# The first block's normalisation moved behind its transposes: x turned by TensorE as it lands, the tokens' scale and bias spread by products with diagonals

## The chip, the core and the metric

The kernel runs on one core of one Trainium2 chip. Five engines work side by side, each through its own list of instructions in a fixed order: TensorE (PE; its weight loads are shown as PEld), VectorE (DVE), ScalarE (ACT), GpSimd (POOL) and SyncE (SP), which here issues most of the transfers. The metric is device time in microseconds (us) of one execution. Three runs of the kernel before gave 2379.66, 2381.79 and 2385.01 us; the median is 2381.79.

## The reference

Two layers over x of shape (2, 4096, 512), float32. Each layer normalises x over its 512 channels and adds the results of two branches to x:

```
xn = (x - mean(x)) / sqrt(var(x) + 1e-5)                     # per token
x1 = xn @ w1.T + w1_b ;  v = silu(xn @ v1.T + v1_b)          # layer 0
y  = ssm(silu(depthwise_conv3(x1)))
x  = x + (y * v) @ w2.T + w2_b + mx_quantised(xn) @ mx_quantised(weight).T + bias
xn = normalised(x)                                           # layer 1
x  = x + linear_attention_with_layernorm(xn) + token_mix_ffn(xn)
```

The change lies at the very beginning: the normalised x of the first 512 tokens, and its first two products, with w1 and v1.

## The kernel before

The 8192 tokens are worked in `NK` = 16 blocks of `T` = 512. Channels are held in `CC` = 4 chunks of 128 partitions, tokens of a block in `TJ` = 4 tiles of 128.

**Phase 1** (`block_kernel`, L1013 to L1102) runs over the 16 blocks. For each, `projected` (L345) makes 32 products of 128x128 weights with 128x512 of `xnT`, the block's normalised x with channels on partitions: four output chunks for w1, then four for v1, four products each, that is over the four channel chunks. In the trace each float32 product of this kind is two entries, so a block is 64 entries. The results go to PSUM banks taken in turn by the generator `banks` (L84) from three tags: `acc` (4 banks), `mm` (2) and `tr` (2), eight in all. ScalarE empties them: L357 adds w1's bias, L372 applies silu with v1's bias. VectorE and ScalarE then do the convolution's taps (`tapped`, L400: L403, L405, L412, L414) and, beside this, the quantisation of other tiles (`quantised`, L384). After phase 1 follow the recurrence and, for each of the two sequences, the mixing of layer 0 and all of layer 1.

**How xnT is made.** For blocks 1 to 15, x is loaded a second time in another layout (`laid`, L317, tile `xi`); ScalarE normalises it in 16 pieces of 128x128 (`laid_normalised`, L173, recorded at L134, four pieces for each 128 tokens), and VectorE transposes it 32 by 32, one instruction for each 128 tokens (L330). The mean and the reciprocal deviation come from the plain x (`fetched`, L292, ten tiles in a ring): `measured` (L299) runs BN_STATS and BN_AGGREGATE over four tiles and a chain of small instructions (L114 to L122, L146), with one square root on ScalarE (L116). `spread_out` (L136) brings these numbers into the other layout: one store to DRAM (`sd`) and four loads (`mvi`). All of a block's xnT has to be there before its first output chunk is complete.

For block 0 there is no time for that way. `first_turned` (L305) normalises the plain tiles on VectorE (L310, four instructions), TensorE transposes them (`transposed`, L150, sixteen transposes into four banks, L154), and ScalarE copies the four banks to xnT (L155).

**What sets the order.** The source is not the order of execution. A scheduler of the framework puts the instructions into one list per engine by its own estimates; each list is then strictly in order, and an instruction that waits holds up all behind it. `tc.issue_after(i)`, used in the change, forces what is issued under it to stand behind instruction i. Transfers on SP's queue also wait for an earlier transfer that used the same of eight semaphores.

In the lists of the kernel before, ScalarE has, after the first block's four w1 evictions: five of block 1's sixteen L134 pieces, the silu of v1's chunk 0, two pieces, chunk 1's silu, six pieces, chunk 2's silu, three pieces, a square root, and only then chunk 3's silu. VectorE has the four transposes of block 1 (L330) between BN_STATS of the x tiles of blocks 3, 4 and 5; those wait for transfers that SP issues late.

## Time and profile before

| | |
|---|---|
| median of the runs | 2381.79 us (2379.66 to 2385.01) |
| the profiled execution's own time | 2385.64 us |
| its span | 2383.8 us |
| TensorE busy | 2353.4 us, 99% of the span |
| VectorE, ScalarE, GpSimd busy | 1530.4, 1012.4, 479.2 us |
| TensorE's first transpose | at 9.73 us |
| TensorE's first product of block 0 | at 14.05 us |
| its last of block 0 ends | at 43.57 us |
| its first of block 1 | at 45.43 us |

Times in the timeline are microseconds from the start of the span: start, length, engine, line, operation, output and inputs, shape, number of instructions in the row; in brackets, how long the engine had been idle and what ended that. PEld rows are weight loads; products follow one another at the spacing of their loads. A row "SPq" or "ACTq" is the issue of a transfer, not the transfer. Because TensorE is busy 99% of the span, what matters is where it is not: the list of waits below is read for TensorE alone.

### The profile page before, as it was taken

Reading aid. Unit: us, or ns where it says so; the run is one execution under the profiler, and the core shown is the slowest. Engines: PE = TensorE matmul, PEld = TensorE weight load, DVE = VectorE, ACT = ScalarE, POOL = GpSimd, SP = SyncE. Lnnn points to the kernel's source line nnn. Section 1 sums busy time; section 2 is a strip of 40 time slices with the busy share of each in tenths; the row PEclk is TensorE's granted clock in tenths of the full one; section 3 lists DMA queues with packets and bytes.
Section 4 is the critical chain, followed back from the end, with each engine's and each line's share of the span. In section 5 each row is a group of like instructions: output and inputs, shape, how many; then the busy total and the mean of one; then the engine's idle time right before and its main releaser. Section 6 shows DMA issues by size and latency. Waiting matters only on the chain. (4 is left out here: it accounts for less than half of the span.)

```text
span 2383.8 us, 21961 instructions
## 1 busy us (share of the span) xinstructions
PE 2353.4 (99%) x6400; PEld 1104.5 (46%) x6400; DVE 1530.4 (64%) x3050; ACT 1012.4 (42%) x1929; POOL 479.2 (20%) x534
## 2 busy tenths in 40 slices
PE   7999999999999999999999999999999999999999
PEld 3444434466444444444445555444444444445554
DVE  6898765554576554266769779666553265567777
ACT  5785675344333233236663222233333246652222
POOL 0121210121243332100112112233332100001111
PEclk9999999999999999999999999999999999999999
DMA  7954433568734432212274445434332212254331
GB/s 246 303 138 142 142 133 115 158 198 288 290 107 119 115 110 86 62 44 97 93 252 164 141 141 194 154 111 120 111 117 65 62 40 80 97 212 142 129 132 57
DMA packets 253833, 328.12 MB, mean 138 GB/s; under 512 B 55953, under 2 KB 117393, under 8 KB 252689
## 3 DMA queue, kind: packets, MB, share of 16 engines
q1 hardware_dynamic: 224624, 259.59, 34.7%
q10 hardware_dynamic: 29088, 67.12, 7.2%
q8 instruction: 51, 0.84, 0.2%
q14 instruction: 70, 0.57, 0.1%
HBM read 205.38 MB, written 121.27 MB: 137 GB/s over the span
## 5 line engine op out<-in xcount | busy, mean ns | idle before, releaser
L704 PE MATMUL p_acc<-k,x 128*128 128x512 f32 x512 | 229.9, 592 | 0.9 <-ACT k L739 0.9
L160 PE MATMUL p_acc<-w_W_v,t 128*128 128x512 f32 x512 | 222.3, 592 | 0.0
L160 PE MATMUL p_acc<-w_W_r,xnT 128*128 128x512 f32 x448 | 201.4, 592 | 0.0
L160 PE MATMUL p_tr<-w_Wk,xnT 128*128 128x512 f32 x448 | 199.2, 592 | 0.1
L977 POOL TENSOR_TENSOR x<-x,row_beta 128x512 f32<-128x512 f32 x64 | 83.9, 1311 | 552.7 <-ACT xn L134 542.6
L673 PE MATMUL p_mm<-w_w_w,t 128*128 128x512 f32 x416 | 186.7, 592 | 0.0
L116 ACT ACTIVATE rs_s<-rs_v 128x4 f32<-128x4 f32 (+1 forms) x41 | 8.3, 205 | 393.7 <-DVE rs_v L114 393.6
L658 PE MATMUL p_mm<-w_d,t 128*128 128x512 f32 x384 | 173.6, 593 | 1.4 <-DVE x L681 1.2
L702 POOL TENSOR_TENSOR ksum<-ksum,k 128x512 f32<-128x512 f32 x62 | 83.3, 1344 | 369.2 <-ACT k L739 369.2
L704 PEld LDWEIGHTS p_acc<-k,x 128*128 128x128 f32 x512 | 97.2, 190 | 123.7 <-issue 120.8
L160 PEld LDWEIGHTS p_acc<-w_W_v,t 128*128 128x128 f32 x512 | 97.3, 190 | 122.5 <-issue 119.3
L738 DVE TENSOR_TENSOR k<-p_tr,row_bk 128x512 f32<-128x512 f32 x64 | 43.8, 684 | 162.1 <-PE p_tr L160 162.1
L983 ACT ACTIVATE r<-p_acc 128x512 f32<-128x512 f32 x64 | 38.2, 597 | 248.3 <-PE p_acc L160 236.3
L405 DVE SCALAR_TENSOR_TENSOR xc<-x,col_conv_w,xc 128x512 f32<-128x512 f32 x128 | 95.7, 763 | 65.8 <-ACT xc L403 33.5
L160 PEld LDWEIGHTS p_tr<-w_Wk,xnT 128*128 128x128 f32 x448 | 85.0, 190 | 107.6 <-issue 104.0
L186 POOL TENSOR_TENSOR xq<-xq,mx_rs 128x512 f32<-128x512 f32 x64 | 76.4, 1194 | 268.6 <-DVE mx_rs L185 205.7
L739 ACT ACTIVATE k<-k 128x512 f32<-128x512 f32 x64 | 40.1, 627 | 202.9 <-DVE k L738 198.5
L673 PEld LDWEIGHTS p_mm<-w_w_w,t 128*128 128x128 f32 x416 | 79.0, 190 | 99.5 <-issue 99.5
L134 ACT ACTIVATE xq<-xq,mvi 128x128 f32<-128x128 f32 x256 | 104.2, 481 | 44.0 <-DMA xq<-in_xi 43.0
L160 PE MATMUL p_acc<-xnT,w_w_w 128*128 128x512 f32 x256 | 117.3, 601 | 4.6 <-ACT x L357 2.1
L681 DVE TENSOR_TENSOR x<-x,p_mm 128x512 f32<-128x512 f32 x52 | 35.5, 683 | 133.3 <-PE p_mm L673 133.2
L160 PEld LDWEIGHTS p_acc<-w_W_r,xnT 128*128 128x128 f32 x448 | 80.8, 190 | 80.4 <-issue 80.4
(235 smaller groups left out, 4375.7 us busy)
## 6 DMA issues: line engine op xcount, KB each, us to landing
x<-in_x SPq DMA_DIRECT2D x126, 256.0 KB, 3.6
xq<-in_xi SPq DMA_DIRECT2D x64, 256.0 KB, 4.4
vd<-v ACTq DMA_DIRECT2D x64, 256.0 KB, 2.4
cd<-xs SPq DMA_DIRECT2D x64, 256.0 KB, 2.0
xg<-cd SPq DMA_DIRECT2D x16, 1024.0 KB, 6.8
v<-vd SPq DMA_DIRECT2D x64, 256.0 KB, 4.6
xd<-x SPq DMA_DIRECT2D x64, 256.0 KB, 2.0
qd<-q ACTq DMA_DIRECT2D x64, 256.0 KB, 2.0
```

The costliest lines, as they stand in the source:

```text
L134: nc.scalar.activation(dst, src, AF.Identity, bias=mv[:, 0:1], scale=mv[:, 1:2])
L160: nc.tensor.matmul(out_ap, lhsT=lhsT(k), rhs=rhs(k), start=(k == 0), stop=(k == CC - 1))
L186: nc.gpsimd.tensor_tensor(by_block(y), by_block(y), rs.unsqueeze(2).to_broadcast([P, NQ, QB]), ALU.mult)
L405: nc.vector.scalar_tensor_tensor(xc, x1[:, cc, tap : tap + T], conv_w[:, cc, tap : tap + 1], xc, ALU.mult, ALU.add,)
L658: nc.tensor.matmul(po, lhsT=xds[i][j][:, k, :], rhs=wd[:, k, :], start=(k == 0), stop=False)
L673: nc.tensor.matmul(po, lhsT=z[:, k, j * P : (j + 1) * P], rhs=w2[:, k, :], start=False, stop=(k == CC - 1),)
L702: nc.gpsimd.tensor_tensor(ksum, ksum, kt, ALU.add)
L704: nc.tensor.matmul(pg[c], lhsT=xn[:, c * P : (c + 1) * P], rhs=kt, start=first, stop=last)
L738: nc.vector.tensor_tensor(kt, pk, bk, ALU.add)
L739: nc.scalar.activation(kt, kt, AF.Relu)
L977: nc.gpsimd.tensor_tensor(xt[j], xt[j], beta, ALU.add)
L983: nc.scalar.activation(r, pr, AF.Sigmoid)
```

## The change

For block 0 alone, the order of normalising and transposing is turned round. TensorE transposes the plain x tiles as they land, into the four `acc` banks, one for each channel chunk. The tokens' scale and bias now have to vary along the free axis, the same on all partitions. They are made so by products: identity times a token's scale on its partition (a diagonal, made on VectorE for the scale and on ScalarE for the bias), multiplied from the left by a matrix of ones, gives a 128x512 tile whose every row holds the 512 tokens' values. ScalarE copies the scale's tile to SBUF; the bias's stays in a `tr` bank. VectorE then multiplies and adds chunk by chunk, eight instructions over 128x512, and forces the order multiply, add, multiply, add. The first two w1 outputs of block 0 are accumulated in turns, channel chunk by channel chunk. The order of bank tags in `banks` changes for all of phase 1, and the two small mask reductions are put behind the last of the eight instructions.

```diff
-            for tag in ("acc", "mm", "acc", "tr"):
+            for tag in ("mm", "tr", "acc", "acc"):
                 yield bank(tag, 4 if tag == "acc" else 2)
...
     def first_turned(work, xts):
         xnT = work.tile([P, CC, T], F32, tag="xnT", name="xnT")
-        xn = work.tile([P, TJ, D], F32, tag="xi", name="xn")
+        pxs = [acc() for _ in range(CC)]
         for j in range(TJ):
-            nc.vector.tensor_scalar(
-                xn[:, j, :], xts[j], mv0[:, 0, j, 1:2], mv0[:, 0, j, 0:1], ALU.mult, ALU.add
-            )
-        for j in range(TJ):
-            transposed(xnT[:, :, j * P : (j + 1) * P], xn[:, j, :], ("tr", "mm")[j % 2])
-        return xnT
+            for c in range(CC):
+                nc.tensor.transpose(
+                    pxs[c][:, j * P : (j + 1) * P], xts[j][:, c * P : (c + 1) * P], ident
+                )
+        measured(0, xts)
+        full = work.tile([P, P], F32, tag="xe", name="full")
+        nc.gpsimd.memset(full, 1.0)
+        wide = {}
+        for k, tag in ((1, "mm"), (0, "tr")):
+            diagonal = work.tile([P, TJ, P], F32, tag="xi", name="diagonal")
+            wide[k] = bank(tag)
+            for j in range(TJ):
+                if k:
+                    nc.vector.tensor_scalar(
+                        diagonal[:, j, :], ident, mv0[:, 0, j, k : k + 1], None, ALU.mult
+                    )
+                else:
+                    nc.scalar.activation(
+                        diagonal[:, j, :], ident, AF.Copy, scale=mv0[:, 0, j, k : k + 1]
+                    )
+                nc.tensor.matmul(
+                    wide[k][:, j * P : (j + 1) * P], lhsT=full, rhs=diagonal[:, j, :],
+                    start=True, stop=True,
+                )
+        scale = work.tile([P, T], F32, tag="xe", name="scale")
+        nc.scalar.copy(scale, wide[1])
+        shifted = None
+        for c in range(CC):
+            with tc.issue_after(shifted.ins) if c else nullcontext():
+                nc.vector.tensor_tensor(xnT[:, c, :], pxs[c], scale, ALU.mult)
+            shifted = nc.vector.tensor_tensor(xnT[:, c, :], xnT[:, c, :], wide[0], ALU.add)
+        return xnT, shifted
...
     def projected(work, n, xnT, before):
...
+        if not n:
+            two = [next(eight) for _ in range(2)]
+            for k in range(CC):
+                for o in range(2):
+                    nc.tensor.matmul(
+                        two[o], lhsT=w1[:, k, o * P : (o + 1) * P], rhs=xnT[:, k, :],
+                        start=(k == 0), stop=(k == CC - 1),
+                    )
         for o in range(CC):
-            pm = next(eight)
-            product(pm, lambda k: w1[:, k, o * P : (o + 1) * P], lambda k: xnT[:, k, :])
+            if not n and o < 2:
+                pm = two[o]
+            else:
+                pm = next(eight)
+                product(pm, lambda k: w1[:, k, o * P : (o + 1) * P], lambda k: xnT[:, k, :])
...
-            measured(0, xts[0])
-            xnT = first_turned(work, xts.pop(0))
+            xnT, shifted = first_turned(work, xts.pop(0))
...
-            nc.vector.tensor_reduce(mask, ...)     # two reductions, mask and mask_c
+            with tc.issue_after(shifted.ins):
+                nc.vector.tensor_reduce(mask, ...)
```

The lists that result differ from those before in phase 1 alone; from the recurrence on, each engine's list holds the same instructions in the same order. What is new in the lists around the first two blocks:

- VectorE: four diagonals; multiply, add for chunks 0 and 1; multiply for chunk 2, one BN_STATS of block 1, add; multiply for chunk 3, BN_AGGREGATE, a second BN_STATS of block 1, add; then the rest of block 1's statistics, with the masks among them. The fourth transpose of block 1 stands behind BN_STATS of the fourth x tile of block 4 and the first two of block 5.
- ScalarE: four diagonals, the copy of the scale, then the first w1 eviction, the square root for block 1, the other w1 evictions and taps, the square root for blocks 2 and 3, and then: silu of v1's chunk 0, one of block 1's sixteen pieces, silu 1, six pieces, silu 2, five pieces, silu 3, four pieces.
- TensorE: sixteen transposes, four products for the scale, four for the bias, then for each channel chunk one product for each of the first two outputs, with one product of the third output ahead of channel chunk 3's.
- SP: the transfers of x for block 3 stand around the store of block 1's statistics and ahead of its four loads. The stores and loads of the statistics of blocks 2 and 3 come ahead of most x tiles of blocks 4 and 5.
- GpSimd: one more memset ahead of the making of the identity.

More of the change, by code (lines that the diff above doesn't have):

```diff
@@ L1 @@
 from collections import defaultdict
-from contextlib import ExitStack
+from contextlib import ExitStack, nullcontext
 from functools import partial
@@ L1036, in block_kernel @@
             mask = const.tile([P, QC], F32, name="mask")
-            nc.vector.tensor_reduce(
-                mask, ident.rearrange("p (q t) -> p q t", q=QC), AX.X, ALU.add
-            )
             mask_c = const.tile([P, QC], F32, name="mask_c")
-            nc.vector.tensor_reduce(
-                mask_c, ident.rearrange("p (u q s) -> p q u s", u=2, q=QC), AX.XY, ALU.add
-            )
+            with tc.issue_after(shifted.ins):
+                nc.vector.tensor_reduce(
+                    mask, ident.rearrange("p (q t) -> p q t", q=QC), AX.X, ALU.add
+                )
+                nc.vector.tensor_reduce(
+                    mask_c, ident.rearrange("p (u q s) -> p q u s", u=2, q=QC), AX.XY, ALU.add
+                )
             x1 = None
```

## The prediction

> **What bounds the kernel now.** I read the page's first part, then TensorE's list of waits, then the timeline of the first 46 us, where the change lies.

> ```profile
> PE 2353.4 (99%) x6400; PEld 1104.5 (46%) x6400; DVE 1530.4 (64%) x3050; ACT 1012.4 (42%) x1929; POOL 479.2 (20%) x534
> ```

> TensorE is busy all the span: a gain must be a gap that TensorE loses, a loss one that it gets. Its gaps are few (line, who released it, us in total, times, longest):

> ```profile
> PE p_tr L154 <- DVE xn L310: 9.7, 1, 9.7
> ...
> PE p_acc L160 <- ACT x L357: 2.1, 1, 2.1
> ...
> PE p_acc L160 <- DVE xnT L330: 1.9, 1, 1.9
> ...
> PE p_acc L160 <- ACT xnT L155: 0.7, 1, 0.7
> ```

> The change works on the first, the last and, through block 1, the third. The second belongs to a group of four waits between 304 and 332 us (0.55, 0.17, 0.22 and 2.06, together 3.0), where ScalarE empties banks so late that all eight are full.

> ```profile
> 8.39 0.28 DVE L1037 TENSOR_REDUCE mask<-ident 128x4 f32<-128x128 f32 x1
> ...
> 9.04 1.91 DVE L310 TENSOR_SCALAR xn<-x,mv 128x512 f32<-128x512 f32 x4
> ...
> 9.73 1.09 PE L154 MATMUL p_tr<-ident,xn 128*128 128x128 f32 x4 [9.73 <-DVE xn L310]
> ...
> 13.41 0.59 ACT L155 COPY xnT<-p_mm 128x512 f32<-128x512 f32 x1 [0.27 <-PE p_mm L154]
> ...
> 14.05 5.48 PE L160 MATMUL p_acc<-xnT,w_w_w 128*128 128x512 f32 x8 [0.68 <-ACT xnT L155]
> ...
> 15.06 0.69 DVE L129 BATCH_NORM_STATS2 st<-x 128x6 f32<-128x512 f32 x1 [4.10 <-DMA x<-in_x]
> ...
> 16.78 0.34 PEld L160 LDWEIGHTS p_acc<-xnT,w_w_w 128*128 128x128 f32 x1 [0.52 <-issue]
> ...
> 17.63 0.21 PEld L160 LDWEIGHTS p_acc<-xnT,w_w_w 128*128 128x128 f32 x1 [0.52 <-issue]
> 18.08 0.19 PEld L160 LDWEIGHTS p_acc<-xnT,w_w_w 128*128 128x128 f32 x1 [0.24 <-issue]
> 18.51 0.19 PEld L160 LDWEIGHTS p_acc<-xnT,w_w_w 128*128 128x128 f32 x1 [0.24 <-issue]
> ...
> 39.97 3.60 PE L160 MATMUL p_tr<-xnT,w_v_w 128*128 128x512 f32 x8
> 40.17 0.69 ACT L372 ACTIVATE v<-p_acc,col_v_b 128x512 f32<-128x512 f32 x1 [0.30 <-PE p_acc L160]
> ...
> 44.70 0.68 DVE L330 STREAM_TRANSPOSE xnT<-xi 128x512 f32<-128x512 f32 x1
> ...
> 45.43 3.70 PE L160 MATMUL p_acc<-xnT,w_w_w 128*128 128x512 f32 x8 [1.86 <-DVE xnT L330]
> ```

> To be seen: product entries follow each other every 0.855 us (16.78 to 17.63) until some 17.9, then every 0.43. TensorE starts at half rate, though the granted clock shown for these stretches is 1.00; I go by the spacing. Block 0 is 64 entries: at 0.429 they take 27.46, and the half-rate time from 14.05 to 17.9 adds half of 3.85, so 14.05 + 27.46 + 1.93 + 0.1 = 43.5 (seen: 43.57). Block 1 waits 1.86 more: its last transpose stands in VectorE's list behind BN_STATS that wait for x tiles.

> **The change, part by part.**

> *Start of block 0.* Removed from the path: L310, the transposes behind it, the copies. The sixteen transposes now wait only for x (first BN_STATS at 4.60) and the identity (1.68, plus 0.20 for the added memset on GpSimd); at the old spacing, 0.215 each, they end near 8.1, beside the statistics, which take until 9.0. Cost nothing; without that cover they would cost their 3.4. Moving the two masks out of the chain of small VectorE instructions brings 0.1: 8.9.

> VectorE's four diagonals (128x128): the rows nearest are a TENSOR_SCALAR of 128x64 at 0.19 and L310's 128x512 at 0.48. I take 0.2, nearer in size; the first is done at 9.1 and TensorE starts at 9.25. Each of the eight products is float32, so two entries, of 128 columns: a quarter of 0.855, 0.21 at half rate, 0.11 at full. The scale's four end at 9.25 + 1.71 = 10.96, the bias's at 12.67 (at full rate 1.7 earlier; with 0.48 diagonals 0.5 later). ScalarE's diagonals cost 0.40 each by L134's 128x128 pieces, 9.0 to 10.6: beside TensorE's work. Copy of the scale: 0.59, to 11.65. Multiply and add have the row of another float32 product and sum out of PSUM:

> ```profile
> L738 DVE TENSOR_TENSOR k<-p_tr,row_bk 128x512 f32<-128x512 f32 x64 | 43.8, 684 | 162.1 <-PE p_tr L160 162.1
> ```

> 0.684 each. Chunk 0: multiply 11.67 to 12.35, add from 12.75 (the bias's products) to 13.43. First w1 entry: 13.5, against 14.05. So the gain at the start is 0.55, not the 5 us by which the transposes move.

> Chunks 1, 2 and 3 follow at 14.85, 16.7 and 18.65: 1.35 each, plus one BN_STATS (0.66, and up to 0.4 of waiting, its tile landing at 15.06) ahead of chunk 2's add and of chunk 3's. TensorE needs 3.4 for a chunk's two products at half rate (four entries) and 1.7 at full, so while cold it is behind the chunks: no stall. Were it warm from the start, chunk 3 would leave 50 entries for after 18.65: end at 40.6, the lower bound for block 0.

> *The clock.* Unknown: when full rate comes. Before, the transposes had been running from 9.73 and the change of spacing still came only 3.85 after the first true product. I take the same moment, 17.9. Then block 0 ends at 13.5 + 27.46 + 2.2 + 0.1 = 43.26, 0.3 earlier than 43.57. Latest bound: twice that half-rate time, 7.7 from 13.5, and an end of 44.9.

> [...]

> *Start of block 1: the added wait.* In the new list ScalarE has four of block 1's sixteen pieces behind the last silu of block 0, and that silu waits for block 0's last product. Before, no piece stood there. So from the end E of block 0: silu starts at E + 0.04 and holds ScalarE 0.59 (40.17 to 40.76); four pieces, 0.51 for the first (a transfer is issued behind it), 0.40, 0.40, 0.48: E + 2.4; VectorE's fourth transpose 0.69; to TensorE 0.05: E + 3.2, against 1.86 before. With E = 43.26: 46.45, against 45.43. **Loss 1.0.** Queued behind these pieces are block 2's sixteen and block 1's first eviction; 6.4 + 1.6 us of them bring that eviction to 53, and TensorE, with eight banks, needs its bank only a block later.

> Were E as early as 40.6, another wait would end last: the fourth transpose stands behind BN_STATS of three x tiles. Their transfers are issued behind the statistics of blocks 2 and 3. By my reckoning: first eviction 23.2; square root; block 1's statistics 25.4 (before 24.99); the x tiles of block 3 by 31; square root 32.1; statistics of blocks 2 and 3 33.2 (before 48.3); eight loads to 39.2; tiles issued to 40.5, landing some 3 later. The transpose can't start before 44.2: TensorE at 45.0, a gain of 0.4. With E = 44.9, 48.1: a loss of 2.7. So −0.4 to +2.7 here.

> *VectorE's load*: eight times 0.684 and four times 0.2, less 1.91: 4.4 us more before 20, where VectorE idles 19 of the first 45. Nothing, if cover remains (third rival).

> *SP*: two x tiles of block 2 now wait for transposes too (done at 8.1, issued at 14). The four x tiles of block 3 cost about 0.45 each ahead of block 1's loads; these wait for their store to land anyway.

> *The rest of phase 1.* Bank tags rotate over the same eight banks: nothing. The lists differ up to some 330 us, and the 3.0 of waits there may vanish or double; the same pile-up of quantisation ahead of silus and evictions stands in the new list, so I take 0, bounds −3.0 and +3.0. Afterwards the lists are equal and everything shifts.

> **Sum** against the profiled execution's 2385.64 (span 2383.8): −0.3 + 1.3 + 0 = +1.0. That execution is 3.85 above the median of the runs, as slow as their slowest, so the change is put on the median: 2381.79 + 1.0 = 2382.8.

> **Rivals.** *First (slower): block 1 waits for a transfer.* The square root of blocks 2 and 3 now stands ahead of block 0's first silu and of all sixteen pieces, and needs four x tiles. I have them by 31; the slowest x transfer in the first 60 us took 9.5 from issue to landing, 6 more than I assume. Then the square root comes at 38, the tiles ahead of the fourth transpose 6 later, at 50, and TensorE starts block 1 at 51.4: +6.0, 2387.8. It decides from 3 us of lateness on, where ScalarE's chain (silus, pieces and issues, 9.2) outlasts block 0. For it: TensorE's start then hangs on two landings in a row. Against: the median landing there was 4.8, and these transfers meet few others.

> *Second (faster, or the same): the gain is kept.* Full rate comes with the diagonals' products, block 1 starts at 45.0, and the new order is rid of the four waits: −0.4 − 3.0 = −3.4, 2378.4. Against: two independent strokes of luck.

> *Third: VectorE's 4.4 us are not covered.* At 304 to 332 TensorE waits for evictions that hang on VectorE; if that lateness has piled up since the start, the whole 4.4 arrives there, and block 1's gap is absorbed by it: 2386.2. Against: VectorE is busy for only 4.30 of the 10 us from 70 to 80.

> That the change doesn't do what it says is excluded: the transposes head TensorE's new list and wait for x and the identity alone.

> **How the numbers follow.** 0.2%, 4.8 us, is about what a measurement of this kernel can tell; the three runs shown spread over 5.4. Forecast 0.60 (own range 2380.5 to 2385.5), first rival 0.14, second 0.12, third 0.14. Faster by over 0.2% (under 2377.0): 0.05 from the second, 0.02 from the forecast. Slower (over 2386.6): 0.11, 0.05 and 0.02 from the first, third and forecast: 0.18. Same: 0.75. The range goes to the second's and the first's price, 2378.4 to 2387.8.

> **What would show it.** Right: transposes from 4.6 to 8.1, a gap, products at 9.3, first w1 entry near 13.5 with spacing 0.855; then block 1 released by the fourth transpose, ScalarE's four pieces directly ahead. Wrong: half spacing gone before 14; a wait for x ahead of the first silu; TensorE's waits of 304 to 332 gone or grown.

## The result, and the profile after

Five runs of the changed kernel took 2393.93 to 2397.61 us, median **2396.7**; the kernel before, on the same chip, 2381.79. The ratio is 1.0057, 95% interval 1.0047 to 1.0068: slower by 14.9 us, 9 over the top of the range on record. The profiled executions stand 8.3 apart only (2393.93 against 2385.64): the one of the changed kernel is the fastest of its five, that of the kernel before lies 3.9 above its median. So the account below is of 8.3 us, and what a slower execution of the changed kernel adds is read from a second profile.

The page's first part of the changed kernel, and TensorE's list of waits (us in total, times, longest us):

```profile
PE 2359.3 (99%) x6416; PEld 1108.9 (46%) x6416; DVE 1539.8 (64%) x3058; ACT 1013.9 (42%) x1931; POOL 476.7 (20%) x535
```

```profile
PE p_acc L313 <- DMA x<-in_x: 4.7, 1, 4.7
PE p_mm L160 <- DVE mv L130: 4.3, 1, 4.3
PE p_mm L160 <- DVE xnT L358: 4.3, 1, 4.3
...
PE p_acc L160 <- ACT x L397: 2.6, 2, 2.1
...
PE p_tr L160 <- ACT x L397: 1.1, 1, 1.1
```

Two waits of 4.3 us are new. The timeline says where they lie (start, length; in brackets the idle time before and what ended it):

```profile
4.71 3.65 PE L313 MATMUL p_acc<-ident,x 128*128 128x128 f32 x16 [4.71 <-DMA x<-in_x]
...
9.11 2.08 PE L332 MATMUL p_mm<-diagonal,full 128*128 128x128 f32 x8 [0.75 <-DVE diagonal L325]
...
13.68 1.13 PE L387 MATMUL p_mm<-xnT,w_w_w 128*128 128x512 f32 x2 [0.78 <-DVE xnT L342]
...
42.23 0.69 DVE L129 BATCH_NORM_STATS2 st<-x 128x6 f32<-128x512 f32 x1 [0.73 <-DMA x<-in_x]
...
43.55 0.69 DVE L129 BATCH_NORM_STATS2 st<-x 128x6 f32<-128x512 f32 x1 [0.41 <-DMA x<-in_x]
...
44.96 0.69 DVE L358 STREAM_TRANSPOSE xnT<-xi 128x512 f32<-128x512 f32 x1
...
45.71 6.05 PE L160 MATMUL p_mm<-xnT,w_w_w 128*128 128x512 f32 x8 [4.29 <-DVE mv L130]
```

The start is as drawn. TensorE then runs out of block 0 at 41.42 (45.71 less 4.29) and waits: the fourth transpose of block 1 stands behind statistics whose x tiles are still landing. (The list names L130, which ends 0.06 us behind the transpose.) The eight entries after the wait need 6.05 us instead of 3.7. In the same execution's windows, the column after POOL is the granted clock:

```profile
40.00:45.00 5.00, 1.41 (x4) 0.34 (x2) 3.00 (x7) 4.26 (x11) 0.00 (x0) 0.86 0.93 307
45.00:50.00 5.00, 4.29 (x5) 1.85 (x6) 4.77 (x14) 5.00 (x14) 0.00 (x0) 0.50 1.03 365
50.00:60.00 10.00, 10.00 (x24) 4.52 (x23) 8.44 (x20) 7.81 (x18) 1.36 (x3) 0.98 0.95 334
```

Behind the gap the clock stood at half, from 43.64 to 50.47 by its record, and behind the second gap again, from 217.72 to 221.14. That gap is at block 7, on VectorE (first fence before, second after):

```profile
202.01 0.67 DVE L182 TENSOR_REDUCE mx_s<-w_y 128x16 f32<-128x512 f32 x1
...
205.01 2.48 DVE L330 STREAM_TRANSPOSE xnT<-xi 128x512 f32<-128x512 f32 x4
...
208.00 0.38 DVE L194 TENSOR_SCALAR w_c<-w_y 128x512 int32<-128x512 int32 x1
```

```profile
207.88 1.25 DVE L194 TENSOR_SCALAR w_c<-w_y 128x512 int32<-128x512 int32 x1
...
209.14 0.67 DVE L182 TENSOR_REDUCE mx_s<-w_y 128x16 f32<-128x512 f32 x1
...
213.13 1.25 DVE L194 TENSOR_SCALAR w_c<-w_y 128x512 int32<-128x512 int32 x1 [0.94 <-POOL w_y L186]
214.42 0.43 DVE L197 TENSOR_SCALAR w_c<-w_c 128x512 f32<-128x512 f32 x1
214.76 2.48 DVE L358 STREAM_TRANSPOSE xnT<-xi 128x512 f32<-128x512 f32 x4
```

Before, one instruction on the tiles `w_y` and `w_c` (the quantisation of the weight for the mixing of layer 0, hundreds of us away) stood ahead of block 7's four transposes; in the new list seven do, with a wait for GpSimd among them. Four other transposes of VectorE that nothing needs so soon (table `ta`, see a_free) moved nearer to block 7 as well, from 182 to 195 us to 193 to 206. Block 6 ends at 213.12 and block 7 cannot begin:

```profile
217.39 5.37 PE L160 MATMUL p_mm<-xnT,w_w_w 128*128 128x512 f32 x8 [4.27 <-DVE xnT L358]
223.81 3.70 PE L160 MATMUL p_tr<-xnT,w_w_w 128*128 128x512 f32 x8 [1.06 <-ACT x L397]
227.99 7.13 PE L160 MATMUL p_acc<-xnT,w_w_w 128*128 128x512 f32 x16 [0.47 <-ACT x L397]
...
340.90 7.13 PE L160 MATMUL p_acc<-xnT,w_w_w 128*128 128x512 f32 x16 [2.10 <-ACT x L397]
```

The account of the profiled pair, after less before: block 0 ends 2.15 earlier (41.42 against 43.57); block 1 starts 0.28 later (45.71 against 45.43); half rate behind the gap, 6.05 − 3.7 = 2.4 by 51; at block 7, 4.27 + 1.06 + 0.47 of waits and 1.7 of half rate, 7.5; the four waits at 304 to 332 (3.0) are one of 2.10, −0.9. Sum 9.3. The recurrence's first products come at 476.21 against 467.07, **+9.14**; from there the lists are equal, and 0.8 comes back.

### The profile page after: what moved, and what is told of

Read it like the earlier page. It is cut to its first block, busy times and chain, and to the rows that moved or that the text cites. A ratio compares the mean times of both kernels' runs of the same rounds, so it can differ in the third digit from the quotient of the medians.

```text
span 2392.1 us, 22005 instructions
## 1 busy us (share of the span) xinstructions
PE 2359.3 (99%) x6416; PEld 1108.9 (46%) x6416; DVE 1539.8 (64%) x3058; ACT 1013.9 (42%) x1931; POOL 476.7 (20%) x535
## 4 chain that ended last, share of the span: by engine, by line
PE 69%; DVE 4%; issue 1%; ACT 1%; POOL 1%; DMA 0%; POOLq 0%; ACTq 0%; DVEq 0%
PE p_acc L160 18%; PE p_tr L160 9%; PE p_acc L744 8%; PE p_mm L713 7%; PE p_mm L698 7%; PE p_mm L869 6%; PE p_acc L869 6%; PE p_tr L869 2%; PE p_mm L996 1%; PE p_tr L996 1%; PE p_acc L698 1%; PE p_acc L534 1%; PE p_acc L713 1%; PE p_acc L544 1%; PE p_tr L713 1%
## 5 line engine op out<-in xcount | busy, mean ns | idle before, releaser
L160 PE MATMUL p_acc<-w_W_v,t 128*128 128x512 f32 x512 | 222.3, 592 | 0.0
L160 PE MATMUL p_acc<-w_W_r,xnT 128*128 128x512 f32 x448 | 201.4, 592 | 0.0
L160 PE MATMUL p_tr<-w_Wk,xnT 128*128 128x512 f32 x448 | 199.2, 592 | 0.2 <-ACT xnT L155 0.2
L160 PEld LDWEIGHTS p_acc<-w_W_v,t 128*128 128x128 f32 x512 | 97.3, 190 | 122.5 <-issue 119.3
L778 DVE TENSOR_TENSOR k<-p_tr,row_bk 128x512 f32<-128x512 f32 x64 | 43.8, 684 | 162.1 <-PE p_tr L160 162.1
L445 DVE SCALAR_TENSOR_TENSOR xc<-x,col_conv_w,xc 128x512 f32<-128x512 f32 x128 | 94.1, 752 | 69.1 <-ACT xc L443 35.9
L160 PEld LDWEIGHTS p_tr<-w_Wk,xnT 128*128 128x128 f32 x448 | 85.0, 190 | 107.7 <-issue 104.0
L134 ACT ACTIVATE xq<-xq,mvi 128x128 f32<-128x128 f32 x256 | 105.2, 481 | 43.7 <-DMA xq<-in_xi 41.6
L160 PEld LDWEIGHTS p_acc<-w_W_r,xnT 128*128 128x128 f32 x448 | 80.8, 190 | 80.4 <-issue 80.4
L160 PE MATMUL p_acc<-xnT,w_w_w 128*128 128x512 f32 x256 | 113.0, 593 | 2.6 <-ACT x L397 2.6
```

What stands on the lines that cost most here:

```text
L134: nc.scalar.activation(dst, src, AF.Identity, bias=mv[:, 0:1], scale=mv[:, 1:2])
L160: nc.tensor.matmul(out_ap, lhsT=lhsT(k), rhs=rhs(k), start=(k == 0), stop=(k == CC - 1))
L445: nc.vector.scalar_tensor_tensor(xc, x1[:, cc, tap : tap + T], conv_w[:, cc, tap : tap + 1], xc, ALU.mult, ALU.add,)
L778: nc.vector.tensor_tensor(kt, pk, bk, ALU.add)
```

## The experiments

All experiments were timed beside the kernel before (medians 2382.7 to 2383.2 on those chips). "Marker" is the start of the recurrence's first product in the one profile of each kernel, to be held against 467.07 before and 476.21 after. That profile is one execution; what a kernel costs is read from the median. The profiled execution of the kernel before took 2385.64, 3.9 above its median, so a marker 2 or 3 us ahead of 467.07 is no gain by itself.

| kernel | median us | ratio to before (95%) | marker |
|---|---|---|---|
| changed | 2396.7 | 1.0057 (1.0047 to 1.0068) | 476.21 |
| a_again | 2398.7, one run | | 480.67 |
| a_t7 | 2392.16 | 1.0038 (1.0025 to 1.0052) | 473.76 |
| a_b1 | 2389.12 | 1.0025 (1.0014 to 1.0037) | 471.73 |
| a_both | 2387.64 | 1.0021 (1.0012 to 1.0030) | 470.68 |
| a_free | 2381.08 | 0.9989 (0.9980 to 0.9999) | 461.94 |
| a_late | 2381.74 | 0.9995 (0.9986 to 1.0003) | 464.45 |
| b_turns | 2383.59 | 1.0003 (0.9994 to 1.0012) | 466.18 |
| b_b1 | 2383.72 | 1.0001 (0.9992 to 1.0010) | 464.25 |
| b_turns_b1 | 2385.98 | 1.0013 (1.0004 to 1.0022) | 467.29 |
| b_late | 2382.17 | 0.9995 (0.9986 to 1.0003) | 464.72 |
| b_turns_b1_late | 2382.47 | 1.0002 (0.9993 to 1.0011) | 464.82 |
| b_b1_late | 2383.92 | 1.0004 (0.9995 to 1.0013) | 463.68 |

Names with a_ start from the changed kernel, with b_ from the one before.

**a_again: the changed kernel once more, unedited.**

> The changed kernel once more, to see how much of its loss is the same in another profiled execution. If the loss is made by the lists (block 1's wait of 4.29 us and block 7's of 4.27, each followed by a stretch at half rate), both waits come back within 0.5 us and the half rate after them in stretches of one or two windows of 3.41 us; the time is 2393 to 2398. If they were an accident of that one execution, one of the two is missing and the time is nearer to 2385.

2398.7 us. TensorE's timeline of this execution:

```profile
9.14 1.16 PE L332 MATMUL p_mm<-diagonal,full 128*128 128x128 f32 x8 [1.15 <-DVE diagonal L325]
12.50 1.13 PE L387 MATMUL p_mm<-xnT,w_w_w 128*128 128x512 f32 x2 [1.31 <-DVE xnT L342]
47.61 5.78 PE L160 MATMUL p_mm<-xnT,w_w_w 128*128 128x512 f32 x8 [7.02 <-DVE mv L130]
220.39 6.41 PE L160 MATMUL p_mm<-xnT,w_w_w 128*128 128x512 f32 x8 [5.64 <-DVE xnT L358]
```

Full rate came while the transposes ran (sixteen in 3.25 us instead of 3.65, by which it came near 7.5 us, an estimate), the scale's products took 1.16 us instead of 2.08, block 0 ended at 40.59, and yet block 1 began at 47.61: the three tiles ahead of the fourth transpose landed later (VectorE waited 1.28, 0.95 and 0.55 for them). Both gaps are there again, so they are the change's own; but the expected 0.5 us was missed: they are 7.02 and 5.64 here, 4.1 more together than in the first profile, whose execution was 4.8 faster.

**a_t7: the weight's quantisation behind block 7's transposes.** `tails[n]` is the last transpose of block n.

```diff
                     if what == "w":
-                        quantised_weight(work, j)
+                        with tc.issue_after(tails[7].ins):
+                            quantised_weight(work, j)
...
```

> The changed kernel with VectorE's share of the quantisation of ffn_weight queued behind the last transpose of block 7; nothing else is forced. Theory: the four transposes of block 7 were late (214.76 us) because the new list puts six weight-quantisation instructions and their waits for GpSimd ahead of them, in a stretch where VectorE is busy for 26 of 27 us. Then the wait of 4.27, the half rate after it (1.7) and the two waits for banks behind it (1.06 and 0.47) go: 7 us less than the changed kernel, ratio to before about 1.003. Rival: the 4.4 us that the change adds to VectorE before 20 us arrive at block 7 whatever the order; then TensorE still waits 3 us or more there and less than 3 us are won.

2392.16, 4.5 less, between what the theory (7) and the rival (under 3) expected. The transposes' wait is gone, but one of 3.91 for an eviction (L397) stands at 222.01 with half rate behind it (6.57 us for eight entries): the work taken from ahead of the transposes is now ahead of a convolution tap of VectorE (L445, 217.10), for which ScalarE waits 11.47 us, with the eviction behind it in its list. Moving this one work gives back a third of the loss, and VectorE is late there with or without it.

**a_b1: the statistics of three tiles behind block 1's fourth transpose.**

```diff
         for j in range(n):
-            nc.vector.bn_stats(st[:, j, :], xt(j))
-            nc.vector.bn_aggr(mv[:, j, :], st[:, j, :])
+            with tc.issue_after(behind.ins) if behind and j >= 3 else nullcontext():
+                nc.vector.bn_stats(st[:, j, :], xt(j))
+                nc.vector.bn_aggr(mv[:, j, :], st[:, j, :])
...
```

`behind` is `tails[1]` in the call for blocks 4 and 5, and nothing elsewhere.

> The changed kernel with BN_STATS of the fourth x tile of block 4 and of block 5's four queued behind the last transpose of block 1. Theory: the gap ahead of block 1 is then ScalarE's silu and four pieces and a transpose, 3.2 us from the end of block 0, instead of 4.29; at 3.2 the clock is not taken down, so 1.1 + 2.4 = 3.5 us are won by block 1's end. The list around block 7 changes as well (three weight instructions ahead of its transposes instead of six), so part of block 7's 7 us may go too; it is read from the waits. Rival: the clock falls after 3.2 us as well, then only 1.1 are won at block 1.

2389.12, 7.6 less. Block 0 ended at 40.71 and block 1 began at 43.93:

```profile
43.93 3.70 PE L161 MATMUL p_mm<-xnT,w_w_w 128*128 128x512 f32 x8 [3.22 <-DVE xnT L359]
```

3.22 is ScalarE's path (the last silu, four pieces, the transpose), which the prediction had at E + 3.2, and behind it the entries run at full rate. At block 7 there are waits of 1.98 and 2.50 in place of 4.27 and 1.06: forcing the order at block 1 changed the list there too, so this run does not price block 1 alone.

**a_both: the two together.**

> Both orders forced at once. Theory: 3.5 + 7 us less than the changed kernel, that is within 2 us of the kernel before (ratio 0.999 to 1.002): the change of block 0 itself is then worth its 2.2 us at the end of block 0, of which the gap ahead of block 1 takes back 1.3. Rival: other waits take the place of these two, and the ratio stays above 1.003.

2387.64: 9.1 less than the changed kernel (the two alone gave 4.5 and 7.6, so they overlap), and 4.9 over the kernel before (ratio 1.0021). The rival held in part: the remaining waits are small and many:

```profile
191.25 3.70 PE L161 MATMUL p_acc<-xnT,w_w_w 128*128 128x512 f32 x8 [0.41 <-ACT x L398]
195.89 3.70 PE L161 MATMUL p_acc<-xnT,w_w_w 128*128 128x512 f32 x8 [0.93 <-ACT x L398]
199.78 3.70 PE L161 MATMUL p_mm<-xnT,w_v_w 128*128 128x512 f32 x8 [0.20 <-ACT v L413]
219.35 3.70 PE L161 MATMUL p_tr<-xnT,w_w_w 128*128 128x512 f32 x8 [2.13 <-ACT x L398]
230.85 3.70 PE L161 MATMUL p_mm<-xnT,w_v_w 128*128 128x512 f32 x8 [0.47 <-ACT v L413]
```

All are evictions by ScalarE between 190 and 231, where VectorE is busy for 25.98 of the 27 us from 183 to 210:

```profile
183.00:210.00 27.00, 25.46 (x59) 10.73 (x58) 25.98 (x36) 10.89 (x19) 9.09 (x12) 1.00 0.40 130
```

The link is ScalarE's list: it stands 10.97 us behind a tap of VectorE, and the evictions stand behind that. In the kernel before a like wait (10.16) is over at 209.54 and TensorE doesn't notice it; here it lasts until 215.93:

```profile
215.93 0.63 ACT L453 ACTIVATE xc<-xc 128x512 f32<-128x512 f32 x1 [10.97 <-DVE xc L446]
```

The next two runs ask whether it is VectorE's crowd that makes them late.

**a_free: a_both without four 128x1024 transposes of VectorE.** `chunk_tables` makes a table `ta` from `kr`, which GpSimd first reads at 454; the transposes stand at 190 to 203. Here `ta` is left zero (one memset of 3.47 us at 1.7 us), so the output is not the reference's.

```diff
-        nc.vector.transpose(
-            window(ta[:, cc, 0, L - 1 : L], [[-1, L], [L, L]]),
-            window(kr[:, cc, 0:1], [[1, L], [1, L]]),
-        )
...
```

> The changed kernel with both orders forced (as in a_both), and VectorE freed of the four 128x1024 transposes that make the table ta (2.0 us each, near 190 to 205 us): the table is zero instead, so the recurrence's output is not the reference's. Theory: what is left of the loss in a_both is VectorE's lateness in blocks 5 to 7; with 8 us less for VectorE there, the waits for banks between 190 and 231 us (4.1 us in a_both's profile) go, and the time is 3 to 4 us less than a_both's. Rival: those waits come from ScalarE's or GpSimd's own queues; then less than 1 us is won.

2381.08. Of the five waits one remains (0.89 at 196.5), and TensorE is never idle between 200 and 467 for a wait that its timeline shows. So 7.8 us of VectorE's work (four times 1.94) in this place were worth 6.6.

**a_late: a_both with these four transposes later**, behind block 12's last transpose, at 335 to 344, where VectorE has room. Nothing left out.

```diff
+                if n == 12:
+                    with tc.issue_after(tails[12].ins):
+                        for dst, src in late:
+                            nc.vector.transpose(dst, src)
...
```

> The changed kernel with both orders undone (a_both), and chunk_tables' four 128x1024 transposes, which VectorE does at 190 to 202 us and GpSimd first reads at 454, put behind block 12's last transpose (some 370 us), where VectorE is busy for 60% of its time. Nothing is left out. Theory (what stayed of the loss in a_both is VectorE's lateness between 183 and 220, by work that isn't due there): the waits of 191 to 231 go as they did without these transposes (a_free): 2381 us, 5 to 7 below a_both's 2387.6. Rival (a_free gained because VectorE had less to do in all, and the work will make evictions late wherever it stands): new waits beyond 304, and 2385 to 2388.

2381.74, 5.9 under a_both and level with the kernel before. ScalarE's wait for the tap is 5.01 us, ending at 208.88. Behind the start of block 1 (first line) TensorE waits twice until 467:

```profile
44.26 5.40 PE L161 MATMUL p_mm<-xnT,w_w_w 128*128 128x512 f32 x8 [3.19 <-DVE xnT L359]
190.79 7.35 PE L161 MATMUL p_acc<-xnT,w_w_w 128*128 128x512 f32 x16 [0.37 <-ACT x L398]
199.03 3.70 PE L161 MATMUL p_mm<-xnT,w_v_w 128*128 128x512 f32 x8 [0.89 <-ACT v L413]
```

With three orders forced, and every instruction of the change left in, the whole loss is gone: **the change's own instructions cost nothing that can be measured (the interval is some 2 us either way) once VectorE's list is in another order.** The first two moves gave back 9.1 of the loss, the third the rest. The third takes the four transposes out of a place into which the new list had pushed them 11 us further; in the kernel before the same move is worth nothing (next run). The rival, that VectorE's work costs wherever it stands, fell.

**b_late: the same move in the kernel before.**

> The kernel before with the same four transposes (there at 182 to 195 us) behind block 12's last transpose. TensorE has no wait between 183 and 300 there, only 3.0 us in four waits at 304 to 332. If these four hang on lateness that VectorE has carried from the crowded stretch: 2380, 3 under before. If they hang on the work of 265 to 332 itself: 2383, as before. Either way the gain must be smaller than in the changed kernel, if it is the change that made VectorE's lateness reach TensorE at block 5 to 7.

2382.17, 0.9995: no difference that can be told. The four waits at 302 to 330 are still there (0.28, 0.16, 0.42 and 1.23). In the kernel before VectorE's crowd is as dense (26.44 of 27 us busy from 183 to 210), but nothing of it reaches TensorE between 46 and 300. So there the margin was enough; how much was left is not shown by TensorE's list of waits, and was not measured. Held against this kernel, which has the same move, a_late is 0.4 away: level here too. (a_t7's move was not tried in the kernel before.)

**b_turns: the kernel before with 24 unused transposes of plain x as it lands** (the early turning alone).

```diff
+            spare = [acc() for _ in range(CC)]
+            for r in range(6):
+                for c in range(CC):
+                    nc.tensor.transpose(spare[c][:, 0:P], xts[0][r % TJ][:, c * P : (c + 1) * P], ident)
             measured(0, xts[0])
```

> The kernel before with 24 more transposes of the first block's plain x on TensorE, from the landing of x (4.7 us) until the first true transpose (9.7), written to acc banks that nobody reads. They compute nothing that is used. Theory: transposes alone bring the clock to full rate (two executions of the changed kernel had it at 7.5 us, when nothing but transposes had run), so block 0 runs at full rate from its first entry and ends 1.9 us earlier, near 41.6; block 1 is gated by its own chain (VectorE's last transpose at 44.7) and starts near 45.4 all the same, the wait ahead of it grows from 1.86 to 3.8, and if the clock falls in it, 1 to 2 us are lost: 0 to +2 us against before. Rival 1: transposes don't count, then products are 0.855 apart until 17 or later and nothing changes. Rival 2: an earlier end of block 0 is kept: -1.9 us.

```profile
4.69 5.20 PE L1025 MATMUL p_acc<-ident,x 128*128 128x128 f32 x24 [4.69 <-DMA x<-in_x]
9.73 0.60 PE L154 MATMUL p_tr<-ident,xn 128*128 128x128 f32 x4
...
12.47 1.98 PE L160 MATMUL p_acc<-xnT,w_w_w 128*128 128x512 f32 x4 [0.83 <-ACT xnT L155]
```

The kernel's own four transposes at 9.73 take 0.60; before, at the same moment, 1.09. Nothing but transposes had run. Block 0 ends at 40.20, 3.4 earlier; then a gap of 3.31 ahead of block 1, the clock at 0.50 from 44 to 47, and 2.62 and 0.27 of eviction waits at 214 to 224. 2383.59: nothing won. The early end of block 0 is given back.

**b_b1: the kernel before with the statistics of blocks 4 and 5, from the fifth tile on, behind block 1's fourth transpose, and b_turns_b1: both.**

> The kernel before with BN_STATS of block 5's four x tiles queued behind the last transpose of block 1 on VectorE; else its lists stay as they are. Theory: the wait ahead of block 1 (1.86) is made by that order; without it the transpose follows ScalarE's last piece (42.15) and block 1 follows block 0 without a gap: 1.9 us earlier at block 1, and 1.9 less in all if nothing later takes it back. Rival: the waits for banks at 304 to 332 (3.0 us) are VectorE's and ScalarE's lateness, which does not come earlier; then they grow by what was won, and the time is as before within 0.5 us.

> Both of the two kernels above in one: the clock raised early by 24 unused transposes, and block 1's last transpose ahead of block 5's statistics. Theory: block 0 ends near 41.6, block 1 starts near 43.5: 1.9 us earlier than in the kernel before, and the clock stays up: -2 us. With the rival of the run above, nothing is won.

b_b1: the gap ahead of block 1 is 0.44 instead of 1.86, the median 2383.72, as before. b_turns_b1: block 1 begins at 40.72, 4.7 before the old 45.43, and the recurrence at 467.29, with the old 467.07; in between TensorE waits at 70, 212 to 221 and 294 to 308, 8.3 in all. 2385.98: slower by some 3 (1.0013, interval 1.0004 to 1.0022). Phase 1 takes back what its start wins.

**b_turns_b1_late and b_b1_late: these two with the four transposes late.**

> The kernel before with the unused turns, the later statistics ahead of block 1 (b_turns_b1) and the four table transposes behind block 12's last transpose (b_late). In b_turns_b1 TensorE began block 1 at 40.7 us, 4.7 earlier than in the kernel before, and had lost all of it by 467 us, in waits at 70, 212 to 221 and 294 to 308. Theory (phase 1 is paced by VectorE's list, so that an early start pays only if that list is lightened too): the waits from 212 on go or halve, 2378 to 2380 us, 3 to 5 under before. Rival (the waits hang on ScalarE's evictions and transfers, not on VectorE's load): 2384 to 2386, as b_turns_b1.

> The kernel before with the later statistics ahead of block 1 (b_b1) and the four table transposes behind block 12's last transpose (b_late), without the unused turns. Theory (VectorE's list paces phase 1): the gap ahead of block 1 (1.86) stays away and the waits at 211, 223 and 323 to 329 shrink: 2379 to 2381 us. Rival (given back as in b_b1): 2383 to 2384.

2382.47 and 2383.92: no version is faster than the kernel before. In b_turns_b1_late the waits at 212 to 221 fell from 2.26 to 0.48, those at 291 to 306 stayed:

```profile
41.42 3.70 PE L161 MATMUL p_acc<-xnT,w_w_w 128*128 128x512 f32 x8 [0.97 <-DVE xnT L331]
214.60 3.70 PE L161 MATMUL p_acc<-xnT,w_w_w 128*128 128x512 f32 x8 [0.48 <-ACT x L358]
291.59 3.67 PE L161 MATMUL p_acc<-xnT,w_w_w 128*128 128x512 f32 x8 [1.19 <-DVE xnT L331]
297.13 3.70 PE L161 MATMUL p_mm<-xnT,w_w_w 128*128 128x512 f32 x8 [1.87 <-ACT x L358]
305.83 3.70 PE L161 MATMUL p_tr<-xnT,w_w_w 128*128 128x512 f32 x8 [1.56 <-ACT x L358]
```

In b_b1_late not even the first crowd is clear: where b_b1 had waits of 0.68 and 0.47, there is one of 2.29 with half rate behind it, though the four transposes are gone from there. ScalarE had stood 2.51 us behind a transfer of x (at 212.24), as the rival has it:

```profile
215.77 5.40 PE L161 MATMUL p_acc<-xnT,w_w_w 128*128 128x512 f32 x8 [2.29 <-ACT x L358]
```

So the theory held for the first crowd of b_turns_b1_late alone. What holds up 291 to 306 was not tried. The markers of b_b1 and b_b1_late are 2.8 and 3.4 early, but their profiled executions (2381.86 and 2381.64) were each 2 us faster than their medians and that of the kernel before 3.9 slower: markers go with the executions.

## Why the prediction was wrong

*Start of block 0: right.* Turns from 4.71 to 8.36 (put at 4.6 to 8.1), the diagonals' products at 9.11 (9.25), 3.8 us for eight and eight entries (3.4), multiply and add 0.69 each (0.684), the first w1 entry at 13.68 (13.5): a gain of 0.37, put at 0.55.

*The clock: the value was wrong, the bounds held, and a term was missing.* "I take the same moment, 17.9" failed: it was full at 12.9 in the profile by its record (the first two w1 entries, at 13.68, took 1.13 us), and, estimated from the lengths of TensorE's rows, near 7.5 in a_again (sixteen transposes in 3.25 us instead of 3.65), near 12.8 in a_t7 (the bias's products in 1.84 instead of 1.92) and near 17.3 in a_both (two w1 entries from 15.47 took 1.91, two from 17.18 took 1.08). Block 0 ended at 41.42, inside the 40.6 to 44.9 put down. (The lower bound was added up wrong: 50 entries of 0.429 from 18.65 end at 40.2, not 40.6; that the earliest end seen, a_again's 40.59, keeps to it is luck.) Transposes alone had brought full rate in b_turns: the kernel's own four took 0.60 us there against 1.09 before. What was missing: the clock fell again. Where the order ahead of block 1 was left as it was, an early end of block 0 had a longer gap behind it (4.29 in the profile, 7.02 in a_again, 4.81 in a_t7, 3.31 in b_turns, against 1.86), and half rate behind that gap cost 2.4 in the profile. The sum had no such term.

*Start of block 1: both paths were named, and the other one decided.* With E (the end of block 0) = 43.26, 46.45 was forecast by ScalarE's path; in a_both, where the statistics are out of the way and the clock was late (17.3), E was 43.15 and block 1 came at 46.37. In the changed kernel itself, with E = 41.42, the second path ended last: the floor "45.0" named the right thing, three tiles' statistics ahead of the fourth transpose, but had the tiles land too early: 45.71 in the profile, 46.32 in a_t7, 47.61 in a_again. The first rival's late landings are thus half true: not at the square root of blocks 2 and 3, but at the statistics.

*"The rest of phase 1 … I take 0, bounds −3.0 and +3.0": this step failed.* In the profiled pair phase 1 lost 8.9 behind the start of block 1 (9.14 at the recurrence less 0.28): 2.4 by half rate behind block 1's gap and 7.5 at block 7, with 0.9 won at 341. In the medians a_both gave back 9.1 and a_late 15, all of it by the order of VectorE's list. The bounds had been taken from the waits that TensorE's list showed, as if those alone could move. The list of after was read for quantisation ahead of silus and evictions, not ahead of the next block's transposes, where it had grown from one instruction to seven. And the margin had been looked up in the wrong place: "VectorE is busy for only 4.30 of the 10 us from 70 to 80", while from 183 to 210 the profile before has

```profile
183.00:210.00 27.00, 27.00 (x65) 11.93 (x64) 26.44 (x45) 9.69 (x16) 7.69 (x12) 1.00 0.31 90
```

VectorE at 26.44 of 27 with TensorE not waiting once. A second engine was as good as full under the first, and a change of its list there could bring waits that no row had shown.

*Third rival: the right engine, the wrong place and reason.* VectorE's lateness did reach TensorE, at 190 to 231 and not at 304 to 332, by where work stood in the list: a_t7 and a_b1 move it about, and a_late keeps all of the 4.4 us added. Whether the 4.9 us left in a_both come from these 4.4 or from what else is ordered anew was not separated; VectorE is idle for 17.3 of the first 45 us there, which speaks for the order.

*Second rival:* the early clock that it needed did come, and its gain was lost in the gap behind it, as in b_turns.

## What to carry to other kernels

When an edit makes a scheduler order lists anew, compare each engine's new list at the places where the *second* busiest engine is full, and ask of each block's last input what now stands ahead of it; a bound on the unseen part has to come from that engine's margin, not from the waits that the trace happens to show. A faster start is worth only what the next hand-over lets through, and a longer gap can cost twice, as here at block 1: once as a wait (4.29 us, 1.86 before) and once as a slower clock (2.4 us). Work that is due hundreds of us later belongs behind the next block's inputs: a dependency of order on four instructions was worth 5.9 us here.

## What was not expected of the hardware

```profile
44.00:48.00 4.00, 3.74 (x6) 1.69 (x7) 4.00 (x11) 4.00 (x12) 0.00 (x0) 0.68 1.02 376
```

In the profile of the changed kernel the clock's records begin at 12.92, 43.64, 50.47, 217.72 and 221.14: the stretches between are 9, 2, 49 and 1 times 3.41 us. The 3.41 us that ended in the two falls held 2.23 us of TensorE's idle time (40.23 to 43.64) and 3.08 (214.31 to 217.72). Counted in the same steps from the first record, 12.92 here and 17.66 in the kernel before, up to 2370 us, the most idle time that one of them held at full rate without a fall at its end was 1.99 (before, 328.28 to 331.69). The ends of products are modelled, so the hundredths are not sure. In a_late the mean of 0.68 from 44 to 48 puts the fall near 45.5, and the 3.41 us ahead of it held 2.2 of the gap (both estimates from these numbers). Where such steps lay in a_b1 and a_both is not shown, and so neither is what parts the three gaps of 3.2; their lengths (3.22, 3.22 and 3.19) do not.

The same TENSOR_SCALAR of 128x512 integers on VectorE (L194) takes 0.38 to 0.43 us or 1.25, within one execution (208.00 and 200.76 before). Why it is long at times was not tried.
